# The first unit's gate and up stage in a written order for all engines, with the second unit prepared between its pairs

## The chip, the cores and the metric

The kernel runs on one NeuronCore of a Trainium2 chip. Its time is device microseconds of one execution; before the change it is 2628.86 us, the median of three runs (2623.89 to 2630.57). TensorE (PE in the profile) multiplies, VectorE (DVE), ScalarE (ACT) and GpSimd (POOL) work elementwise, SyncE (SP) issues all of the kernel's data transfers. Each engine takes its instructions in one fixed order and waits on semaphores.

## The reference

```python
mod = (_silu(L0_c) @ L0_wmod).reshape(L0_c.shape[0], 6, 1, -1)
sa, ca, ga, sb, cb, gb = (mod[:, 0], mod[:, 1], mod[:, 2], mod[:, 3], mod[:, 4], mod[:, 5])
...
h = _layernorm(x, axis=-1) * (1 + ca) + sa
x = x + ga * _L0_attn_ref(h)          # softmax over the 2 samples, per feature, then a mix of them
h = _layernorm(x, axis=-1) * (1 + cb) + sb
x = x + gb * _L0_ffn_ref(h, W_gate, W_up, W_down)
# ffn: up = xf W_up^T, gate = silu(xf W_gate^T), y = (gate * up) W_down^T
```

x is 2 samples of 2048 tokens of 1024 features; the hidden width is 2752. All is float32.

## The kernel before

The tokens are worked in 8 units of 256 tokens of both samples (512 columns). A float32 matrix product is made of float16 ones: each operand is scaled by a power of two and split into a high and a low part (`split`, L152: `high` on ScalarE or GpSimd, L148 and L150, then the low part on VectorE, L154), and three products of parts are added (`PARTS`). From the second unit on, gate and up and the down product run in seven half-size products instead of eight (`gu_pair`, L860; `DN_STEPS`), on sums and differences of blocks of the weights that are prepared once and kept in DRAM: `dgu` for gate and up, `dwd` for down. The first unit meets weights that are not prepared yet.

**Unit 0, gate and up.** The hidden rows go in 11 pairs (`Pair`; the last is half a pair), each with four blocks: gate and up, each in two halves of the contraction. `gu_plain` (L804) multiplies pair p in four steps of 24 matmuls of 512 columns (12 in the last pair), and after each step calls `tick`. That tick makes a block some steps ahead: `block` (L468) splits it into one of five weight tiles (`wtile`) and stores it to `dgu`, odd blocks with the high part on GpSimd. A pair's blocks are read from DRAM four at a time (`load`), a pair's scale needs the largest sum of squares of its blocks: `sums` (Square on ScalarE, L133), `scale_start` (a VectorE maximum), then `laid_out` (L102), a short matmul pa that spreads the maximum over the partitions, then `scale_end` on VectorE (L107 to L121). When m = 0 is multiplied, Silu is taken (L824), when m = 1 is, the product goes to H (L827), and then the sum of its squares is taken.

The same tick also prepares the down weights (`prep_wd`, a generator, one piece at each call): four tiles m, each with four blocks of 640 KB read into `rot`, eight sums of squares, a scale, seven operands (three plain blocks and four sums or differences by `combine`, L429 to L434), each split in two halves into `wt` and `hp` and stored to `dwd`. It reads and multiplies the last section of wmod (`mod_section`), the left-over hidden rows (`prep_left_over`) and the last down rows (`prep_wd_last`).

**Unit 0, down** (L1068 on). Seven steps of 120 matmuls (dX, dY, dZ, L1085), each on an operand of H that `right_dn` forms and splits on ScalarE and VectorE; the sums go back with `add_to`; then pB. Between the steps the next unit is prepared (`prep`, side): z from the unit's x and the statistics `bct` (L650, L651), the attention result (L665 to L669), a mean over the partitions (GpSimd), the deviations and their squares, a root, h. In the last steps the operands of h for the next unit are made (`right_gu`).

**Order.** The text runs up to the third tick of unit 0 under `manual_schedule` for TensorE, VectorE, ScalarE and GpSimd (`in_text`) and for SyncE (`in_order`): there each engine issues in the order of the text. From then on a planner orders each engine's instructions by modelled times, and `issue_after` holds some back. So in unit 0 from about 140 us the order before is the planner's.

## Time and profile before

| What | us |
|---|---|
| Three runs | 2628.86, 2623.89, 2630.57 |
| Profiled execution, its own time | 2624.7 |
| Its span, first to last instruction | 2622.9 |
| First matmul of the gate and up stage of unit 0 (L818) | 116.35 |
| First matmul of its down stage (L1085) | 368.71 |
| First pB of unit 0 (L1111) | 472.96 |
| Granted clock over the span | 0.991 |

Busy time over the span: PE 2556.6 (97%), PEld 2087.5 (80%), DVE 1600.4 (61%), ACT 982.1 (37%), POOL 136.0 (5%). A matmul's end is modelled and matmuls overlap, so a busy TensorE need not be at its peak: the distance from start to start is what counts. An instruction of VectorE starts some 0.07 us before the one in front of it is booked as ended.

### The profile page before, as it was taken

To read this page: it belongs to the slowest core of one execution; us is meant where nothing else is said; L and a number is where in the kernel's file an instruction comes from. 1 tells how busy PE (TensorE), PEld (TensorE's weight loads), DVE (VectorE), ACT (ScalarE), POOL (GpSimd) and SP (SyncE) were. 2 spreads that over 40 slices of the span, in tenths; PEclk is the share of its full clock that TensorE was granted. 3 is DMA by queue.
4 is the path that set the end of the run, shared out by engine and by line. 5 is a ranking of instruction groups with operands and counts; after the bars stand their busy time and mean duration, and the time that the engine had idled before them with its cause. 6 is when DMAs were issued, how large, how long until landed. Compare 5 with 4: busy or idle time off the path is not lost.

```text
span 2622.9 us, 50756 instructions
## 1 busy us (share of the span) xinstructions
PE 2556.6 (97%) x21729; PEld 2087.5 (80%) x21729; DVE 1600.4 (61%) x2659; ACT 982.1 (37%) x1496; POOL 136.0 (5%) x70
## 2 busy tenths in 40 slices
PE   7899898999999999999999999999999999999999
PEld 3344357788887888888887888878887888888887
DVE  8767579866766777493376626584284825622263
ACT  7767564433432454152242423233141413311230
POOL 6211101000000000000000000000000000000000
PEclk9999999999999999999999999999999999999999
DMA  9988765755568766576656666576666666656654
GB/s 390 359 307 320 281 225 174 258 190 193 183 203 293 252 227 216 194 234 201 200 202 225 205 201 200 197 237 201 185 219 218 205 202 202 200 192 202 201 199 152
DMA packets 159010, 586.62 MB, mean 224 GB/s; under 512 B 17216, under 2 KB 17280, under 8 KB 158784
## 3 DMA queue, kind: packets, MB, share of 16 engines
q1 hardware_dynamic: 158784, 583.38, 65.6%
q8 instruction: 170, 2.79, 0.4%
q14 instruction: 56, 0.46, 0.1%
HBM read 506.47 MB, written 76.84 MB: 222 GB/s over the span
## 4 chain that ended last, share of the span: by engine, by line
PE 81%; DMA 8%; DVE 4%; issue 2%; ACT 1%; SPq 0%; DVEq 0%; ACTq 0%
PE pY L875 19%; PE pZ L875 12%; PE pX L875 12%; PE dY L1085 12%; PE dX L1085 8%; PE dZ L1085 7%; PE g L818 3%; PE g L843 3%; PE pB L1111 3%; PE pl L913 1%; DMA out_dram<-big 1%; DMA dwd<-wt 1%; DMA rot<-in_wgp_dram 1%; DMA big<-in_xT_dram 1%; DMA wo<-dgu 1%
## 5 line engine op out<-in xcount | busy, mean ns | idle before, releaser
L875 PEld LDWEIGHTS <-w 128*128 128x128 f16 x8820 | 861.4, 98 | 106.7 <-DMA w<-dgu 3.9
L1085 PEld LDWEIGHTS <-wd 128*128 128x128 f16 x6720 | 658.8, 98 | 88.1 <-issue 6.6
L875 PE MATMUL pY<-hbt,w 128*128 128x256 f16 x3780 | 442.4, 273 | 0.0
L1085 PE MATMUL dY<-rot,wd 128*128 128x256 f16 x2880 | 320.6, 274 | 0.0
L875 PE MATMUL pX<-hbt,w 128*128 128x256 f16 x2520 | 300.6, 273 | 0.0
L875 PE MATMUL pZ<-hbt,w 128*128 128x256 f16 x2520 | 294.4, 273 | 2.8 <-DMA w<-dgu 2.8
L875 PEld LDWEIGHTS <-wo 128*128 128x128 f16 x2688 | 263.4, 98 | 38.0 <-DMA wo<-dgu 4.6
L150 ACT ACTIVATE rot<-H,sA 128x1024 f16<-128x1024 f32 (+1 forms) x168 | 162.8, 1001 | 232.3 <-PE dY L1085 119.8
L818 PE MATMUL g<-hbt,wq 128*128 128x512 f16 x1008 | 226.4, 385 | 11.1 <-ACT wq L150 8.2
L154 DVE SCALAR_TENSOR_TENSOR rot<-H,sA,rot 128x1024 f16<-128x1024 f32 (+1 forms) x168 | 183.0, 1106 | 75.7 <-ACT rot L150 75.3
L1085 PE MATMUL dX<-rot,wd 128*128 128x256 f16 x1920 | 213.7, 273 | 9.4 <-DVE rot L154 5.0
L1085 PE MATMUL dZ<-rot,wd 128*128 128x256 f16 x1920 | 213.5, 273 | 0.0
L818 PEld LDWEIGHTS <-wq 128*128 128x128 f16 x1008 | 99.1, 99 | 134.2 <-ACT wq L150 9.9
L892 DVE TENSOR_TENSOR ev<-pY,e 128x512 f32<-128x512 f32 (+1 forms) x72 | 47.7, 663 | 254.1 <-PE pY L875 252.9
L133 ACT ACTIVATE junk<-H 128x1024 bf16<-128x1024 f32 (+1 forms) x100 | 98.7, 987 | 163.7 <-DVE H L902 146.1
L897 ACT ACTIVATE sil<-ev,inv_f 128x512 f32<-128x512 f32 (+1 forms) x72 | 50.5, 701 | 244.6 <-DVE ev L895 244.3
L875 PE MATMUL pY<-hbt,wo 128*128 128x256 f16 x1152 | 134.6, 273 | 1.5 <-DVE ev L892 1.0
L665 ACT ACTIVATE o<-big,beta,alpha 128x256 f32<-128x256 f32 x112 | 59.8, 592 | 202.3 <-DVE big L651 180.3
L883 DVE TENSOR_TENSOR ev<-pY,e 128x512 f32<-128x512 f32 (+1 forms) x72 | 47.6, 661 | 124.4 <-PE pY L875 124.4
L886 ACT COPY e<-pZ 128x512 f32<-128x512 f32 (+1 forms) x72 | 40.4, 561 | 188.5 <-PE pZ L875 188.4
L843 PE MATMUL g<-hbt,wo 128*128 128x256 f16 x960 | 108.6, 275 | 2.2 <-DMA wo<-dgu 2.2
L843 PEld LDWEIGHTS <-wo 128*128 128x128 f16 x960 | 94.2, 99 | 15.4 <-DMA wo<-dgu 2.5
(298 smaller groups left out, 2728.1 us busy)
## 6 DMA issues: line engine op xcount, KB each, us to landing
w<-dgu SPq DMA_DIRECT2D x350, 512.0 KB, 4.3
wd<-dwd SPq DMA_DIRECT2D x224, 640.0 KB, 3.9
wo<-dgu SPq DMA_DIRECT2D x85, 512.0 KB, 5.1
dgu<-wo SPq DMA_DIRECT2D x40, 512.0 KB, 4.4
rot<-in_wgp_dram SPq DMA_DIRECT2D x38, 512.0 KB, 5.7
dgu<-wq SPq DMA_DIRECT2D x35, 512.0 KB, 6.4
big<-in_wgp_dram SPq DMA_DIRECT2D x32, 512.0 KB, 7.9
out_dram<-big SPq DMA_DIRECT2D x30, 512.0 KB, 3.1
```

The costliest lines, as they stand in the source:

```text
L133: S.activation(jv, src, AF.Square, accum_out=col)
L150: mark["hi"] = S.activation(dst_hi, src, AF.Copy, scale=s)
L154: return V.scalar_tensor_tensor(dst_lo, src, s, dst_hi, ALU.mult, ALU.subtract)
L665: S.activation(o[:, n], z[:, q, 0], AF.Identity, scale=alpha[:, n, 0, q:q + 1], bias=beta[:, n, q:q + 1])
L818: T.matmul(pt[m, f].rearrange("p n c -> p (n c)"), w[:, wa, f, k], hb0[:, ha, 4 * kh + k], start=kh == 0 and k == 0 and j == 0, stop=kh == ...
L843: T.matmul(pt[m, f][:, n], w[:, wa, f, k], hb[:, ((1, 0), (2, 3))[kh][n], ha, k], start=kh == 0 and k == 0 and j == 0 and n == 0, stop=kh ...
L875: T.matmul(pt[a][:, f], w[:, wa, f, k], hb[:, i, ha, k], start=a not in seen, stop=k == 3 and j == 2, skip_group_check=True)
L883: V.tensor_tensor(u2, pt["Y"], e1, ALU.add)
L892: V.tensor_tensor(c22, pt["Y"], e1, ALU.add)
L897: S.activation(sr, u2, AF.Silu, scale=inv)
L1085: T.matmul(acc[a, h][:, j], w[:, k // 5, wa, k % 5], rot16[:, si % 2, ha, k], start=(a, h) not in seen, stop=k == KH - 1 and jj == 2, skip ...
L1111: T.matmul(pB, wt[0:n, k, wa, m, :], hp[0:n, k, ha, :], start=i == 0, stop=i == len(LAST) - 1)
```

## The change

The text order now holds to the end of the gate and up stage of unit 0, for all five engines: `in_text` and `in_order` are closed after `gu_left_over`, and both `issue_after` at that place go. The work of a tick is written out for step t = 4p + i in `later_tick`, by tables: which block is read (`LOADS`, one a step, each pair in a place of its own, `PLACE`), when the down tiles are read, squared, scaled and split (`T_WD`), when z, y and the deviations of unit 1 are made (`second.z`, `Y0`, `Y1`, `DEV`, `ADD`). So the preparation of unit 1 moves from the down stage into these steps, all but its last part: `rest` (b1, sb) stays in the down stage and the root is taken beside the left-over rows. The last down rows (`prep_wd_last`) move from the gate and up stage into the first two down steps.

Squares are taken over two blocks in one instruction (`sums_of_two`, `Down.sums`), and a down operand is split in one instruction of 1280 elements instead of two of 640, and stored in one transfer of 640 KB, in three places in the spare half of `hbt`. Silu, H and its sum of squares are put off (`late`): Silu to the end of its step's work, H behind the first block of the next pair. Tiles `wt`, `hp` and the small evacuation tiles of `gu_pair` become parts of one tile `mix`, and pairs 5, 7 and 9 are read into it. The sums for the last wmod section are multiplied at the ends of steps 4 to 7, from two places in turn. Units 1 to 7 issue the same instructions as before.

```diff
...
-    hp = ct([P, 2, 2, 2 * TU], "hp", F16)
-    wt = ct([P, 2, 2, KB, P], "wt", F16)
+    mix = ct([P, 4 * D + 3 * 2 * TU], "mix")
+    wt = mix[:, 0:2 * D].bitcast(F16).rearrange("p (a b c d) -> p a b c d", a=2, b=2, c=KB)
+    hp = mix[:, 2 * D:3 * D].bitcast(F16).rearrange("p (a b c) -> p a b c", a=2, b=2)
+    ets = {"sil": [0, 1], "e1": [2, 3], "e5": [4]}
...
+        def sums_of_two(self, i):
+            sumsq(self.base[:, 2 * i * self.n:2 * (i + 1) * self.n], self.sq[:, i:i + 1])
...
+    Hf = H.rearrange("p a n c -> p (a n c)")
+    HT = 2 * TU
+    PLACE = {2: big[:, 1], 3: big[:, 2], 4: Hf[:, 12 * HT:20 * HT], 5: mix[:, 0:4 * D], 6: Hf[:, 12 * HT:20 * HT],
+             7: mix[:, 0:4 * D], 8: Hf[:, 14 * HT:22 * HT], 9: mix[:, 0:4 * D], 10: Hf[:, 18 * HT:22 * HT]}
...
+    class Down:
+        def __init__(self):
+            n = self.n = KH * P
+            self.q = [rot[:, i * n:(i + 1) * n] for i in range(4)]
+            self.place = [spare[:, i * n:(i + 1) * n].bitcast(F16).rearrange("p (g h c) -> p g h c", g=2, h=2)
+                          for i in range(3)]
+            self.at = 0
+        def load(self, m, blocks):
+            for i in blocks:
+                Q.dma_start(self.q[i], wd[m][:, i])
+        def sums(self, i):
+            if i == 0:
+                self.sq = small.tile([P, 2], F32, tag="sqd", name="sqd")
+            sumsq(rot[:, 2 * i * self.n:2 * (i + 1) * self.n], self.sq[:, i:i + 1])
+        def scale_start(self):
+            c = small.tile([P, 1], F32, tag="sqc", name="sqc")
+            V.tensor_reduce(c, self.sq, AX.X, ALU.max)
+            return bound(c)
+        def scale_end(self, m, pa):
+            pow2_end(pa, s_wd, inv_wd[:, m:m + 1])
+        def operands(self, m, ids):
+            for i in ids:
+                w = self.place[self.at % 3]
+                self.at += 1
+                src = self.q[{3: 1, 5: 0, 6: 3, 7: 2, **PLAIN}[i]]
+                split(w[:, :, 0], w[:, :, 1], src.rearrange("p (g c) -> p g c", g=2), s_wd)
+                Q.dma_start(dwd[m, i], w.rearrange("p g h c -> p (g h c)"))
...
+    class Second:
...
+        def z(self, ks):
+            nb = [bct[:, i].rearrange("p n c -> p (n c)") for i in range(2)]
+            for k in ks:
+                V.tensor_tensor(self.zf[:, k], self.xf[:, k], nb[1], ALU.add)
...
+            if kh and m == 0:
                 for f in range(nf):
+                    pt["s", f] = evp.tile([P, 2, TU], F32, tag="ev", name="silp", bufs=3)
+                late.append(lambda: [S.activation(pt["s", f], pt[0, f], AF.Silu, scale=inv) for f in range(nf)])
+            if kh and m == 1:
+                late.append(lambda: [V.scalar_tensor_tensor(H[:, 2 * p + f], pt[1, f], inv, pt["s", f], ALU.mult, ALU.mult)
+                                     for f in range(nf)])
+                late.append(lambda: sumsq(H[:, 2 * p:2 * p + nf].rearrange("p f n c -> p (f n c)"), asq[:, p:p + 1]))
...
+            gu_left_over(u, left.w, asq, between=beside_left_over)
+            in_text.close()
+            in_order.close()
+            side = second.rest()
...
+            if u == 0 and si < 2:
+                next(wd_last)
+                if si == 0:
+                    V.tensor_scalar(cB, gbt, iv[1], None, ALU.mult)
...
+            late.pop(0)()
+            w5.extend(mod_load(5, kk, slots_x[2:4]) for kk in range(2))
         if i == 3:
             for b in range(2, 4):
                 pairs[1].block(b)
+            pairs[3] = Pair(3, None, PLACE[3])
+            pairs[3].load(range(4))
+            for b in range(2):
+                pairs[2].sums_of_two(b)
...
+    T_WD = {9 * m + 4: m for m in range(4)}
+    LOADS = {(1, 4 * (q - 3) + b + 1): (q, b) for q in (4, 5, 6, 7, 9) for b in range(4)}
+    LOADS.update({(1, 21): (8, 3), (1, 22): (8, 0), (1, 23): (8, 1), (1, 24): (8, 2), (1, 31): (10, 0), (2, 31): (10, 1),
+                  (1, 32): (10, 2), (2, 32): (10, 3)})
+    Y0 = {17: (0,), 18: (1,), 23: (2, 3), 24: (4, 5), 25: (6,), 26: (7,)}
+    Y1 = {18: (0,), 23: (1,), 24: (2, 3), 25: (4, 5), 26: (6,), 27: (7,)}
+    DEV = {32: (0, 1), 33: (2, 3), 34: (4,), 35: (5,), 36: (6, 7)}
+    ADD = {33: (1,), 34: (2, 3), 35: (4,), 36: (5,), 37: (6, 7)}
+    def later_tick(p, i, asq, s_h, inv_h, right):
+        t = 4 * p + i
+        if i == 0:
+            close, sums_of_h = late[:2]
+            del late[:2]
+            asqs.append(sums_of_h)
+        for l in (1, 2):
+            if (l, t) in LOADS:
+                q, b = LOADS[l, t]
+                if q not in pairs:
+                    pairs[q] = Pair(q, None, PLACE[q])
+                pairs[q].load((b,))
+        m = T_WD.get(t)
+        if m is not None:
+            down.load(m, (0,))
+        m = T_WD.get(t - 1)
+        if m is not None:
+            down.load(m, (1, 2, 3))
+        if t in (5, 6):
+            w5.append(mod_load(5, t - 3, slots_x[2:4]))
+        if 8 <= t < 12:
+            if t == 8:
+                second.stat()
+            second.load(2 * (t - 8))
...
+        if i == 3 and p + 2 <= NP:
+            bounds[p + 2] = pairs[p + 2].scale_start()
+        if i == 0 and t > 4 and p + 1 <= NP:
+            pairs[p + 1].scale_end(pas.pop(p + 1))
+            pairs[p + 1].inv()
+        if t == 4:
+            bounds[2] = pairs[2].scale_start()
+        if t == 5:
+            pairs[2].scale_end(pas.pop(2))
+            pairs[2].inv()
+            pairs[2].block(0)
+        if t > 4 and p + 1 <= NP:
+            pairs[p + 1].block(i)
+        if i == 0:
+            close()
+        if asqs and (i == 3 or t == 40):
+            asqs.pop()()
+        for t0, m in T_WD.items():
+            if t - t0 == 3:
+                down.sums(0)
+            if t - t0 == 4:
+                down.sums(1)
+            if t - t0 == 5:
+                bounds["wd"] = down.scale_start()
+            if t - t0 == 6:
+                down.scale_end(m, pas.pop("wd"))
+                down.operands(m, (4, 1))
+            if t - t0 == 7:
+                down.operands(m, (2,))
+                combine(down.q, 6)
+            if t - t0 == 8:
+                combine(down.q, 5)
+                down.operands(m, (6, 5))
+            if t - t0 == 9:
+                combine(down.q, 3)
+                down.operands(m, (7, 3))
+        if p + 2 <= NP and i in (1, 2):
+            pairs[p + 2].sums_of_two(i - 1)
+        if 14 <= t < 18:
+            second.z((2 * t - 28, 2 * t - 27))
+        second.y_end(Y1.get(t, ()))
+        second.y_start(Y0.get(t, ()))
+        if t == 27:
+            second.total("mean")
+        if t == 29:
+            second.mean()
+        second.add(ADD.get(t, ()))
+        second.dev(DEV.get(t, ()))
+        if t == 37:
+            second.total("var")
+        if t == 39:
+            second.mean()
+            second.root()
+            second.r = tmp.tile([P, 2 * TU], F32, tag="r2", name="r2")
+        if t == 38:
+            left.sums()
+        if t == 39:
+            bounds["left"] = left.scale_start()
+        if t == 40:
+            left.operand(pas.pop("left"))
+        if t == 8:
+            row_of(5)
+        if t == 10:
+            mod_put(5, pts[5])
+            gate(mods[5])
+        if t == 41:
+            c = small.tile([P, 1], F32, tag="cm", name="cm")
+            V.tensor_reduce(c, asq[:, 0:NP], AX.X, ALU.max)
+            bounds["h"] = bound(c)
+        if t == 43:
+            pow2_end(pas.pop("h"), s_h, inv_h)
+            right()
+        if i == 1:
+            late.pop(0)()
+        if t == 9:
+            turn_of(5)
+        for q in (2, p + 2, "wd", "left") + (("h",) if t == 42 else ()):
+            if q in bounds:
+                pas[q] = laid_out(bounds.pop(q))
+        if t in (4, 5, 6, 7):
+            steps_of(5, w5, (t - 4,))
...
+    def beside_left_over():
+        for j in range(7):
+            second.rsqrt(j)
+            if j == 3:
+                for f in late:
+                    f()
...
-        unit(u, iter(()) if last else prep(u + 1), None if last else right_gu(V))
+        unit(u, iter(()) if last or u == 0 else prep(u + 1), None if last else right_gu(V))
```

## The prediction

> **What bounds the kernel now.** I read first the page, then the matmuls of TensorE in order of time over the first unit, then what TensorE waited for in two stretches, and last the other engines there.
>
> The page's slices of 65.6 us (busy tenths; the last row is the granted clock):
>
> ```profile
> PE   7899898999999999999999999999999999999999
> DVE  8767579866766777493376626584284825622263
> PEclk9999999999999999999999999999999999999999
> ```
>
> TensorE is the bound almost everywhere; the dents are in the first seven slices. The change touches the gate and up stage of unit 0 (116.35 to 369) and its down stage (369 to 473). Busy time there:
>
> ```profile
> 116.35:369.00 252.65, 238.48 (x1107) 108.23 (x1108) 169.79 (x291) 170.63 (x287) 32.70 (x20) 0.97 0.75 278
> 369.00:473.10 104.10, 95.39 (x842) 83.68 (x842) 98.26 (x164) 47.45 (x71) 7.41 (x2) 0.97 0.61 214
> ```
>
> The columns are length, PE, PEld, DVE, ACT, POOL, clock, DMA share, GB/s. In the first stretch VectorE has a third of its time free; in the second it has none. The waits show as gaps between matmul groups (start, length, what, idle before):
>
> ```profile
> 133.81 13.11 PE L818 MATMUL g<-hbt,wq 128*128 128x512 f16 x60
> ...
> 299.99 3.60 PE L818 MATMUL g<-hbt,wq 128*128 128x512 f16 x8 [8.20 <-ACT wq L150]
> 305.16 5.35 PE L818 MATMUL g<-hbt,wq 128*128 128x512 f16 x24 [1.57 <-DVE wq L154]
> 310.35 0.39 PE L102 MATMUL pa<-ident,p2b 128*128 128x128 f32 x2
> 310.57 25.85 PE L818 MATMUL g<-hbt,wq 128*128 128x512 f16 x119
> 336.26 0.39 PE L102 MATMUL pa<-ident,p2b 128*128 128x128 f32 x2
> ...
> 350.63 0.49 PE L102 MATMUL pa<-ident,p2b 128*128 128x128 f32 x2 [3.53 <-DVE p2b L113]
> 351.29 11.36 PE L818 MATMUL g<-hbt,wq 128*128 128x512 f16 x44 [0.17 <-DVE wq L154]
> ```
>
> ```profile
> 400.44 0.39 PE L1085 MATMUL dX<-rot,wd 128*128 128x256 f16 x1 [3.71 <-DMA wd<-dwd]
> 400.85 3.95 PE L1085 MATMUL dY<-rot,wd 128*128 128x256 f16 x24
> 408.74 3.38 PE L1085 MATMUL dX<-rot,wd 128*128 128x256 f16 x21 [3.95 <-DVE rot L154]
> ```
>
> From 310.57 to 336.26 are 119 matmuls, 0.216 us each; a step (one block, 24 of them) is 5.18 us. After the 8.20 wait 8 matmuls took 3.60 instead of 1.73: a long wait is paid twice, in the clock too (it stood at 0.50 from 300 to 304).
>
> **What is removed.** Gate and up: waits 8.20 + 1.57 + 3.53 = 13.3; slow matmuls after them 1.9, and 1.7 in the group at 351.29 (11.19 to the next group, 44 x 0.216 = 9.50). Together **16.9 us**. Down: 840 matmuls at 0.1092 (120 in 13.10) are 91.7; from 368.71 to the first pB at 472.96 it is 104.25, so 12.5 lost and 0.67 in front: **13.2 us**. Its cause is VectorE: preparing unit 1 there costs it z 10.0, y 17.0, the deviation 9.7 and the root 5.5, 42 of its 98 us. These leave the stage and 56 remain for 92. What stays or comes (two splits of wd20/wd21 at 1.27, their Squares on ScalarE, the 0.75 MB read just as the weight tiles are fetched) lies beside TensorE. Should the next weight tile be late behind that read, it costs at most what the 3.71 row shows; at best nothing. I leave 2.5 us, so the gain is **10.7**.
>
> **What is added: a written order.** Step t = 4p + i is block i of pair p. Now each engine takes the 44 steps in the order of the text, and the short matmul that spreads a maximum over the partitions (pa, L102) stands at a fixed place on TensorE. Behind a late pa the whole next pair waits. On VectorE a step t cannot run before TensorE has ended step t-1 (five weight tiles, the fifth is that step's), so it gathers no lead; by the end of step 4p+3 it must have started that step's work. So I count VectorE step by step. Prices, as start to next start: low part of a block 1.20 (row 1.28, 0.07 overlap), H 2 x 0.67, scale begun 0.34, scale ended with its factor 1.0 (210.22 to 211.19), the ScalarE high part that must follow before the low 1.1, z 0.61 each, subtraction of down blocks 1.40.
>
> Three prices have no row. A split of 1280 elements: 640 takes 0.87, 1024 takes 1.27, so between 1.27 and 1.74; the line through both gives 1.54, I take 1.47 net. A Square of 2048 or 2560 on ScalarE: 640 is 0.74 and 1024 is 1.04, so 2.0 and 2.4 with the read of the sum, against 2.4 and 3.4 for the separate ones it replaces: ScalarE gains 0.4 to 1 each time. A GpSimd block beside VectorE work:
>
> ```profile
> 181.62 3.02 POOL L148 TENSOR_SCALAR wq<-big,s_gu 128x1024 f16<-128x1024 f32 x1 [11.45 <-DMA big<-in_wgp_dram]
> 183.66 1.66 DVE L154 SCALAR_TENSOR_TENSOR hp<-rot,s_wd,hp 128x640 f16<-128x640 f32 x1
> ```
>
> The split took 1.66 rather than 0.87, GpSimd 3.02 rather than the 1.12 it shows with VectorE idle. Bounds 0 and 0.8 for each odd block; I take 0.5, since some fall into VectorE's pauses.
>
> The Trainium skill (GPSIMD Engine Reference, Key points) says GpSimd shares its SBUF interfaces with VectorE and contends with instructions that have two SBUF inputs. The trace agrees at 183.66. As nearly all of VectorE's work here has two inputs, the rule alone would charge every odd block 0.8, some 6 us more than I do, and it speaks against this change.
>
> Steps 10 to 15, from the end of step 9: 10: 1.2, down scale 2.0 with its ScalarE wait, two splits 2.9, gate of mods[5] 0.6 = 6.7. 11: 0.3 + 1.7 + 1.5 + 2.8 = 6.3. 12: scale 1.0, wait 1.1, 1.2, H 1.3, 1.4, 2.9 = 8.9. 13: 1.7 + 1.4 + 2.9 = 6.0. 14: 1.2 + z 2.4 = 3.6. 15: 0.3. That is 31.8. In front stands 1.8, and at 14 some 2.7, because ScalarE does its share in order too: Silu of the pair waits for TensorE and the next high part stands behind it. 36.3 against six steps with a pa, 31.3: **5.0** before the pa of pair 5. The same count from the end of step 18 (7.0, 8.9, 6.0, 5.5, 0.3, waits 3.7 = 31.4 against 26.1) gives **5.3** before pair 7's; from 27 (9.6, 6.0, 5.5, 0.3, wait 2.5 = 23.9 against 21.0) **2.9** before pair 9's; at 36 the down scale **1.6**, and **0.8** at 18 and 27 together; from 36 to 39 (7.9, 5.5, 6.4 against 15.8) 4.0 before the pa of the left-over, of which the wait at 36 has given about 1, so **3.0**; at 42 **0.5**. Sum 19.1.
>
> The clock adds 1.8 after each of the two long waits (rows 8.20 and 3.53). For the two near 3 the bounds are 0 (row 1.57) and 1.7; nearest is 3.53, but they are shorter, so 0.8 each. Sum 5.2. The Trainium skill (TensorE: Matmul & The Clock Gate, What's actually happening) puts half clock behind an idle window of about 3.4 us; the 0.50 row agrees, and by it the two short ones would cost nothing, 1.6 less.
>
> A further wait is a **transfer**. The third megabyte tile of wmod is issued at step 5 behind the loads of that step, and TensorE needs it after step 6. SP's order from the first store of pair 1 (137.2 in the trace): 3 stores of 512 KB, 2 x 1024, 4 x 512, 640, 512, 3 x 640, 1024: 9728 KB, 9.96 MB. At the 417 GB/s that the trace holds from 256 to 262 this is 23.9 us, plus 1.4 to land (a 256 KB store takes 2.0, 0.6 of it transfer): 162.5. TensorE is there at 139.0 + 3 x 5.18 + 0.2 + two groups of 1.0 = 156.8. **5.7**, and 1.8 in the clock: 7.5. Bounds 0 and 8; I take 7.5, as the queue is full without a break. The other moved loads (xT and stat at steps 8 to 11, a pair's blocks one a step) wait at the head of SP for VectorE's step before, as the stores do; the median for a block of weights is 7.8 us to land in this stretch, and a block is used two or three steps (10 to 15 us) after its issue, so I cost them at nothing. With a VectorE late by a step that cover is down to 5 us, and ScalarE's Squares would wait the missing 3.
>
> ACT's two table loads (Sqrt, then Silu, 1.28 each) move from the down stage to steps 39 and 41 and lie beside the pa waits already counted. Units 2 to 7 issue the same work; their TensorE waits after 473 (14 us in all) I leave as they are.
>
> **Sum.** -16.9 + 19.1 + 5.2 + 7.5 = +14.9 in gate and up, -10.7 in down: +4.2. The profiled execution took 2624.7 (span 2622.9, 1.8 around it), so 2628.9; the median of the three runs is 2628.86, 4.2 above it, so **2633**. What can be told from no change is 0.3%, 7.9 us: 2621 to 2636.7.
>
> **Rivals.** *VectorE keeps up* (30%). For: its 183 us of work (170 less 19 of overlaps, 291 x 0.065, and 3 of fused splits, plus 35, the 42 without the root and overlaps) fit into 231 of matmuls; a few tenths saved in each step undo the pa waits, since each is a difference of two sums near 30. At 5% less and no GpSimd contention 19.1 + 5.2 falls to about 6: 2633 - 18 = **2615**; without the wait on wmod too, 2608. Against: the same steps carry ScalarE's order, and none is free.
>
> *GpSimd and ScalarE slow VectorE's steps* (27%), the slower side. Place: the splits of steps 10-13, 19-22, 28-31, 37-40. With 0.8 for each odd block VectorE loses 0.15 us more a step, with 3% on the rest another 0.15; over 35 steps 10.5, all of it before a pa, plus 2 of clock: **2646**. It decides as soon as VectorE's sum in a pair passes the 21 us of its four steps; pairs 3, 5 and 7 pass it already.
>
> *The down stage does not gain* (6%): its wait moves to wd tiles behind the wd20 read. For: the 3.71 row is such a wait; against: dwd is written long before now. +4 to +8, 2637 to 2641.
>
> **Chances.** Forecast 37%, its own range 2624 to 2641: of it 0.31 within 0.3%, 0.06 slower. First rival 0.28 faster, 0.02 within; second 0.26 slower, 0.01 within; third 0.04 slower, 0.02 within. Faster 0.28, same 0.36, slower 0.36. The range runs from the first rival's lower end, 2608, to the second with the down loss on top, 2652.
>
> **What would show it.** Right: TensorE waits "pa <- DVE p2b" several times in 200-380, one "pm <- DMA wmod" near 157; the first dX some 15 us later than 368.7; the down stage near 94 us to pB, with z, o and acc work before it. Wrong: pa waits under 1 us (then the first rival), the wmod wait absent, or new waits in units 1 to 7 from another order there.

## The result, and the profile after

The changed kernel takes 2649.3 us (median of four runs, 2647.67 to 2651.82), the kernel before beside it 2626.58 (four runs): a ratio of 1.0086, 95% interval 1.0068 to 1.0104. It is slower by 0.9%. The forecast was no change (2633, its own range 2624 to 2641); the time lies outside that and inside the whole range, 2608 to 2652. The second rival (GpSimd and ScalarE slow VectorE's steps, 2646) names the side and the place. The profiled execution took 2648.61, its span is 2646.8.

The page's slices (65.6 us before, 66.2 now; the last row is the granted clock):

```profile
PE   7889889999999999999999999999999999999999
PEclk9999899999999999999999999999999999999999
```

The windows of gate and up and of the down stage of unit 0, from the first matmul of gate and up to the first dX and from there to the first pB (columns as in the prediction):

```profile
116.41:399.70 283.29, 246.31 (x1105) 110.32 (x1105) 212.56 (x326) 168.31 (x200) 35.69 (x22) 0.93 0.72 267
399.70:493.51 93.81, 93.81 (x845) 83.48 (x845) 69.70 (x114) 40.41 (x57) 0.00 (x0) 0.98 0.59 199
```

Between the same instructions, gate and up took 252.36 us before (116.35 to 368.71) and takes 283.29 now, at a clock of 0.93 rather than 0.97. The down stage shrank from 104.25 to 93.81, and TensorE no longer pauses in it (it starts at a slow clock, behind the wait of 2.44 us in front of the first dX). VectorE is busy 212.56 us in the first stage, where it was 169.79: the second unit's preparation has moved there. The 71 us that remain to it are not free, as will be seen.

TensorE's matmuls of the stage in order of time (start, length, what, idle before and who ended it):

```profile
164.81 1.94 PE L196 MATMUL pm<-hbt,csT 128*32 128x512 f32 x8 [6.74 <-DMA hbt<-in_wmod_dram]
...
221.97 0.77 PE L112 MATMUL pa<-ident,p2b 128*128 128x128 f32 x2 [5.05 <-DVE p2b L123]
...
271.51 0.79 PE L112 MATMUL pa<-ident,p2b 128*128 128x128 f32 x2 [5.05 <-DVE p2b L123]
272.10 23.58 PE L928 MATMUL g<-hbt,wq 128*128 128x512 f16 x96
...
322.77 0.80 PE L112 MATMUL pa<-ident,p2b 128*128 128x128 f32 x2 [5.14 <-DVE p2b L123]
...
377.26 0.79 PE L112 MATMUL pa<-ident,p2b 128*128 128x128 f32 x2 [9.19 <-DVE p2b L123]
377.84 10.66 PE L928 MATMUL g<-hbt,wq 128*128 128x512 f16 x36
...
399.70 0.49 PE L1155 MATMUL dX<-rot,wd 128*128 128x256 f16 x3 [2.44 <-DVE H L936]
```

Four waits for pa carry the loss, before pairs 5, 7 and 9 and before the left-over. Each is paid again in the clock: the 96 matmuls after 272.10 take 23.58 us, undisturbed ones 20.88; the 36 after 377.84 take 10.66, where the same 36 take 7.93 in the last run below.

VectorE's busy time in three of the stretches that end in such a wait (length, busy, clock, DMA share, GB/s):

```profile
196.00:221.97 25.97, 22.79 (x26) 0.95 0.87 309
245.60:271.50 25.90, 21.78 (x24) 0.98 0.81 293
296.75:322.77 26.02, 21.69 (x31) 0.98 0.52 201
```

TensorE's four steps are 20.9 us long. VectorE is busy for more than that, and it waits besides, 2.9, 3.9 and 4.0 us in these stretches, nearly all of it for the halves of the splits that ScalarE and GpSimd make (the 4.9 in an expectation below counts one more wait, of 1.0 us, that ends just ahead of the second stretch). The two together are nearly the whole 26 us.

In the stretch before the left-over GpSimd is the one to look at. First its own timeline:

```profile
360.71 3.63 POOL L765 PARTITION_ALL_REDUCE var<-acc  x1 [7.28 <-DVE acc L782]
371.29 0.68 POOL L158 TENSOR_SCALAR wq<-H,s_gu 128x512 f16<-128x512 f32 x1 [6.95 <-issue]
```

Then VectorE's:

```profile
361.15 3.53 DVE L164 SCALAR_TENSOR_TENSOR hbt<-rot,s_wd,hbt 128x1280 f16<-128x1280 f32 x1
...
372.01 0.75 DVE L164 SCALAR_TENSOR_TENSOR wq<-H,s_gu,wq 128x512 f16<-128x512 f32 x1 [4.39 <-POOL wq L158]
```

The all-reduce is shown with 3.63 us, but the block behind it on GpSimd starts 10.58 us after it did, and VectorE waits 4.39 for that block. The split beside the all-reduce takes 3.53 us where most of its shape take 1.55. The other all-reduce, for the mean, starts at 298.75, and GpSimd's next block at 308.88.

What stands between the two is in the rows of the block's line, on GpSimd's own sequencer (POOLq), which do not count as busy:

```profile
L158 POOLq MODIFY_POOL_CONFIG  x2: 98/98/98, 301.9 to 302.0; - x2
L158 POOLq MODIFY_POOL_CONFIG  x2: 98/98/98, 364.3 to 364.3; - x2
```

They come right behind the all-reduces, and each time the block starts 7.0 us later. The result of an all-reduce is out long before that. In the kernel before, where no block and no such row follows, ScalarE reads the mean 4.21 us after its all-reduce began, as it does the variance 3.27 us after (453.86 to 457.13):

```profile
434.50 4.17 POOL L657 PARTITION_ALL_REDUCE mean<-acc  x1 [87.44 <-DVE acc L669]
438.71 0.63 ACT L658 ACTIVATE mean<-mean 128x512 f32<-128x512 f32 x1 [3.91 <-POOL mean L657]
```

So by these rows it is GpSimd's change from the all-reduce back to blocks that holds its queue, and not the all-reduce itself. No run here changes that alone. Where an expectation below says that an all-reduce holds GpSimd for some 10 us, this change is the larger part of it.

### The profile page after: what moved, and what is told of

Read it like the earlier page. It is cut to its first block, busy times and chain, and to the rows that moved or that the text cites. A ratio compares the mean times of both kernels' runs of the same rounds, so it can differ in the third digit from the quotient of the medians.

```text
span 2646.8 us, 50538 instructions
## 1 busy us (share of the span) xinstructions
PE 2566.5 (97%) x21729; PEld 2091.1 (79%) x21729; DVE 1601.0 (60%) x2631; ACT 962.4 (36%) x1384; POOL 131.5 (5%) x70
## 4 chain that ended last, share of the span: by engine, by line
PE 79%; DMA 6%; DVE 4%; issue 1%; ACT 1%; SPq 0%; POOL 0%; DVEq 0%; ACTq 0%
PE pY L985 19%; PE pZ L985 12%; PE pX L985 12%; PE dY L1155 12%; PE dZ L1155 8%; PE dX L1155 8%; PE pB L1185 3%; PE g L953 2%; DMA rot<-in_wgp_dram 2%; PE g L928 2%; PE pl L1023 1%; DMA wl<-dgl 1%; DMA out_dram<-big 1%; DMA w<-dgu 1%; DMA wo<-dgu 0%
## 5 line engine op out<-in xcount | busy, mean ns | idle before, releaser
L985 PEld LDWEIGHTS <-wo 128*128 128x128 f16 x2688 | 264.3, 99 | 40.5 <-DMA wo<-dgu 5.9
L160 ACT ACTIVATE rot<-H,sA 128x1024 f16<-128x1024 f32 x168 | 162.6, 1001 | 238.9 <-PE dY L1155 127.9
L164 DVE SCALAR_TENSOR_TENSOR rot<-H,sA,rot 128x1024 f16<-128x1024 f32 x168 | 182.6, 1100 | 83.8 <-ACT rot L160 83.4
L1002 DVE TENSOR_TENSOR ev<-pY,mix 128x512 f32<-128x512 f32 (+1 forms) x72 | 47.7, 662 | 253.4 <-PE pY L985 252.2
L1007 ACT ACTIVATE mix<-ev,inv_f 128x512 f32<-128x512 f32 (+1 forms) x72 | 50.5, 701 | 246.3 <-DVE ev L1005 245.6
L993 DVE TENSOR_TENSOR ev<-pY,mix 128x512 f32<-128x512 f32 (+1 forms) x72 | 47.6, 661 | 124.1 <-PE pY L985 124.1
L691 ACT ACTIVATE o<-big,beta,alpha 128x256 f32<-128x256 f32 x96 | 51.4, 592 | 195.0 <-DVE big L677 181.3
L1136 DVE SCALAR_TENSOR_TENSOR big<-dY,cA,big 128x256 f32<-128x256 f32 x96 | 41.8, 477 | 113.7 <-PE dY L1155 113.7
L996 ACT COPY mix<-pZ 128x512 f32<-128x512 f32 (+1 forms) x72 | 40.4, 561 | 185.9 <-PE pZ L985 185.8
```

What stands on the lines that cost most here:

```text
L160: mark["hi"] = S.activation(dst_hi, src, AF.Copy, scale=s)
L164: return V.scalar_tensor_tensor(dst_lo, src, s, dst_hi, ALU.mult, ALU.subtract)
L691: S.activation(o[:, n], z[:, q, 0], AF.Identity, scale=alpha[:, n, 0, q:q + 1], bias=beta[:, n, q:q + 1])
L985: T.matmul(pt[a][:, f], w[:, wa, f, k], hb[:, i, ha, k], start=a not in seen, stop=k == 3 and j == 2, skip_group_check=True)
L993: V.tensor_tensor(u2, pt["Y"], e1, ALU.add)
L1002: V.tensor_tensor(c22, pt["Y"], e1, ALU.add)
```

## The experiments

Twelve kernels ran. Ratios are to the kernel before on the same chip, with the 95% interval; the changed kernel's is 1.0086, and 0.001 is 2.6 us. "First dX" is the start of the down stage in the run's profile, 399.70 in the changed kernel; the start of gate and up itself differs between the profiles, from 115.25 to 116.76. The sums of waits for pa are those within gate and up, 25.5 us in the changed kernel (25.6 with one of 0.16 just ahead of it). The intervals of most single runs overlap that of the changed kernel, so there the stage in the profile says more than the median.

**The wmod tiles ahead of the pair's loads in SyncE's queue.**

```diff
@@ first_tick
+            w5.extend(mod_load(5, kk, slots_x[2:4]) for kk in range(2))
         if i == 2:
...
@@ later_tick
+        if t in (5, 6):
+            w5.append(mod_load(5, t - 3, slots_x[2:4]))
         for l in (1, 2):
             if (l, t) in LOADS:
```

> The first two megabyte tiles of the last wmod section are issued right after the stores of pair 0, the third and fourth at the head of steps 5 and 6, ahead of the loads of those steps. Everything else as after the change. Theory (the wait on the third tile is a transfer standing behind 9.7 MB in SP's order): the two waits of 2.2 and 6.7 us and the slow clock behind the second go, about -9 to -11, near 2639; the pa waits stay as they are. Rival (VectorE bounds the stage and used those 9 us to catch up): the pa waits of pairs 4 and 5 grow by what is taken away, -0 to -3, near 2648.

2646.56 us, 1.0068 (1.0053 to 1.0083). The waits for wmod fall from 8.9 to 4.4 us (the first tile is in time, the third still 4.39 late), first dX comes 3.8 earlier (395.89), and the median is 2.7 lower. The waits for pa grow from 25.5 to 28.0 and take part of it back, mostly at the pa of down scales and not at pairs 4 and 5, where the rival had them. The time lies between the two expectations: the tile is a term of its own, and a small one.

**The block behind each all-reduce to ScalarE.**

```diff
-            split(w[:, 0:self.n], w[:, self.n:], self.q[i], self.s, on_pool=i % 2 == 1)
+            split(w[:, 0:self.n], w[:, self.n:], self.q[i], self.s, on_pool=i % 2 == 1 and (self.p, i) not in ((8, 1), (10, 3)))
```

> The high parts of the two odd blocks that stand behind a partition all-reduce on GpSimd (block 1 of pair 8, block 3 of pair 10) go to ScalarE. Theory (GpSimd is held some 10 us by each all-reduce, 360.7 to 371.3 for the second, and the block behind it, then VectorE, then the pa of the left-over wait for it): VectorE's wait of 4.4 us goes, the pa wait of 9.2 falls to 4 to 5, that of pair 9 from 5.1 to about 3.5, -5 to -8 with the clock, near 2643. Rival (the 9.2 is VectorE's own sum of steps 36 to 39): the pa wait stays above 8, less than -2.

2645.23 us, 1.0064 (1.0049 to 1.0079), first dX at 394.82. The pa of the left-over:

```profile
372.36 0.80 PE L112 MATMUL pa<-ident,p2b 128*128 128x128 f32 x2 [5.34 <-DVE p2b L123]
```

It waits 5.34 instead of 9.19, that of pair 9 waits 3.59 instead of 5.14. Two blocks moved off GpSimd's queue are worth some 4 us: what stands behind an all-reduce on GpSimd does come late. The 5 us waits before pairs 5 and 7, which have no all-reduce near, stay (5.06 and 4.81), and small waits before other pa give back 1.4 of the 5.4 us.

**The second unit's preparation back in the down stage.**

```diff
-        if 14 <= t < 18:
-            second.z((2 * t - 28, 2 * t - 27))
...
-            side = second.rest()
...
-        unit(u, iter(()) if last or u == 0 else prep(u + 1), None if last else right_gu(V))
+        unit(u, iter(()) if last else prep(u + 1), None if last else right_gu(V))
```

> The preparation of unit 1 (x and stat loads, z, y, mean, deviations, root) goes back to the down stage, as before the change; the written order, loads and places stay. Theory (two things add up, the lumps of the down weights in a fixed order and the moved work): pa waits are left, 1 to 3 us each for pairs 5, 7, 9 and the left-over, the wmod wait stays, the down stage is back at some 104 us; 2635 to 2643. Rival (the moved work alone makes VectorE too slow): all pa waits under 0.6 us, 2625 to 2630. Rival (the order alone, the moved work fits into pauses): pa waits as after the change, 2657 to 2661.

2666.17 us, 1.0139 (1.0123 to 1.0156): slower than any theory had it, and for a reason that none had. The run does not do what it was made for. VectorE's timeline in gate and up:

```profile
182.00 1.87 DVE L692 SCALAR_TENSOR_TENSOR o<-big,alpha,o 128x256 f32<-128x256 f32 x3 [0.18 <-ACT o L691]
...
262.78 2.15 DVE L164 SCALAR_TENSOR_TENSOR wq<-mix,s_gu,wq 128x1024 f16<-128x1024 f32 x1 [13.27 <-POOL wq L158]
```

L692 is the second unit's preparation. Written behind the ordered text, it belongs to the planner, which put it not into the down stage but early into gate and up, in front of operands that are due; its all-reduces came at 224.97 and 251.65, and VectorE waited 13.27 for the block behind the second. TensorE waited 47.1 us for pa. The question was asked again for part of this work, with its order held, in the last runs below.

**The planner's order from step 4 on**, with all else of the change.

```diff
                 pairs[2].sums_of_two(b)
+            in_text.close()
+            in_order.close()
+            ctx.enter_context(tc.issue_after(mark["h2"].ins))
+            ctx.enter_context(tc.issue_after(last_of_text.ins))
```

> The written order ends where it ended before the change, behind the third tick; the steps, loads, places and moved work stay, and the planner orders each engine from there. Theory (the fixed places of pa and of the wmod sums on TensorE cost the time, not the amount of work): pa waits under 5 us in sum, the down stage stays near 94 us, 2612 to 2632. Rival (VectorE has too much work in this stage, or the transfers come too late, in any order): waits of 20 us and more again, 2640 to 2655.

2652.36 us, 1.0086 (1.0071 to 1.0101): the rival. The written order is not worse than the planner's for this arrangement of the work: the waits only stand elsewhere, as TensorE's timeline shows.

```profile
221.69 34.05 PE L928 MATMUL g<-hbt,wq 128*128 128x512 f16 x151 [7.14 <-DVE wq L164]
...
276.37 0.80 PE L112 MATMUL pa<-ident,p2b 128*128 128x128 f32 x2 [10.82 <-DVE p2c L129]
```

**Each pa one step later.**

```diff
-        if i == 0 and t > 4 and p + 1 <= NP:
+        if i == 1 and t > 5 and p + 1 <= NP:
             pairs[p + 1].scale_end(pas.pop(p + 1))
             pairs[p + 1].inv()
+            pairs[p + 1].block(0)
...
-        for q in (2, p + 2, "wd", "left") + (("h",) if t == 42 else ()):
+        for q in (2, p + 1 if i == 0 else None, "wd", "left") + (("h",) if t == 42 else ()):
```

> Each pair's exponent product pa (pairs 6 to 10) is issued one step of gate and up later, and that pair's operands and three of its loads follow it by a step; the work is the same. Theory: the changed kernel loses its time to exponent products put into TensorE's order before VectorE and ScalarE, which take turns within a step, have the maximum ready (5.05 before pair 5, 5.05 before pair 7, 5.14 before pair 9, 0.53 before pair 8). With a step to spare the waits of pairs 7 to 9 go: 9 to 11 us less gate and up, 2638 to 2641 us. Rival: the engines have too little room in a step, so a wait taken away comes back at the next one, in front of the down operands or of the later operand: within 3 us of the changed kernel, 2646 to 2652 us.

2647.66 us, 1.0084 (1.0069 to 1.0099): the rival. TensorE's timeline has the waits again, at the pa of a down scale, fewer and longer:

```profile
241.16 0.80 PE L112 MATMUL pa<-ident,p2b 128*128 128x128 f32 x2 [7.58 <-DVE p2b L123]
...
297.49 0.80 PE L112 MATMUL pa<-ident,p2b 128*128 128x128 f32 x2 [6.94 <-DVE p2b L123]
```

The sum of the waits for pa is 28.2 us against 25.5. VectorE was not a step late at one place, to be forgiven by a step; it had that much more to do, and the next pa collects it.

**All odd blocks on ScalarE.**

```diff
-            split(w[:, 0:self.n], w[:, self.n:], self.q[i], self.s, on_pool=i % 2 == 1)
+            split(w[:, 0:self.n], w[:, self.n:], self.q[i], self.s)
```

> All odd blocks of the first unit's pairs are scaled on ScalarE in place of GpSimd: 16 to 18 more operations of 1.15 us on ScalarE, and GpSimd is left with the two all-reduces. Theory of the prediction's second rival (GpSimd lengthens VectorE's splits, 1.28 to 1.73 us and 1.55 to 3.5 us where they overlap, and its all-reduce holds the next block some 10 us): VectorE's waits for GpSimd (7.8 us in gate and up) and the lengthened splits go, the wait before the left-over block's product falls from 9.2 to about 5: 2640 to 2645 us. Rival: ScalarE, whose squares end just ahead of each maximum, is the one that is late, and 1.15 us more in every second step makes every product's wait longer: 2650 to 2662 us.

2649.89 us, 1.0089 (1.0073 to 1.0106): within the noise of the changed kernel and at the edge of the rival's range. VectorE's busy time from 180 to 400 falls from 180.39 to 173.58 us and its waits for GpSimd's blocks (10.8 in the changed kernel, counted over these 220 us) go, but VectorE now waits for ScalarE:

```profile
DVE wq L164 <- ACT wq L160: 32.3, 20, 4.2
```

In the changed kernel these are 17.1 us. GpSimd does cost VectorE time, 0.4 us a block by an estimate (6.8 us over the 16 blocks of this window), and ScalarE has none to give for it.

**Less VectorE work, twice.** Both leave operations out. The first run takes 11.0 us off VectorE where the tables put z and y, the second 11.9 us off it in the four stretches in which the down operands are made.

```diff
@@ first run
                 V.tensor_tensor(self.zf[:, k], self.xf[:, k], nb[1], ALU.add)
-                V.tensor_tensor(self.zf[:, k], self.zf[:, k], nb[0], ALU.mult)
...
-                V.tensor_tensor(self.x[:, q], self.x[:, q], o, ALU.add)
@@ second run
             if t - t0 == 8:
-                combine(down.q, 5)
                 down.operands(m, (6, 5))
             if t - t0 == 9:
-                combine(down.q, 3)
                 down.operands(m, (7, 3))
```

> The changed kernel with 16 VectorE operations left out in the preparation of the second unit: the product with the reciprocal root in steps 14 to 17 and the sum of the residual in steps 18 to 27 (8 each of 0.69 us, 11.0 us in all). Its output for that unit is therefore not the reference's. Theory as it stands after the products were moved by a step and only came to wait elsewhere: gate and up of the first unit is now bound by VectorE, whose busy time (180 of 220 us) and its waits for ScalarE's and GpSimd's halves (30 us) fill the stage, so work taken off it comes straight off: 2637 to 2643 us, the waits for products down from 25.6 to about 16. Rival: the places of the products in TensorE's order bind, and each waits for the squares on ScalarE: 2646 to 2650 us.

> The changed kernel with two of the four in-place combinations of each part of the down matrix left out, 8 VectorE operations of 1.48 us, 11.9 us in all; two of each part's seven scaled operands are therefore those of plain blocks, and the output is not the reference's. The amount is that of t1_less_vectore (11.0 us, which moved the median by nothing), but all of it stands in the stretches of four steps (20.9 us) at whose end the products of pairs 5, 7, 9 and of the left-over block wait: there VectorE is busy 22.8, 21.8 and 21.7 us and waits 2.9, 4.9 and 3.9 us for ScalarE's and GpSimd's halves, together about the 26 us that the stretch takes. Theory (VectorE with these waits bounds those four stretches and nothing else): each wait falls by 3.0 us, from 5.05, 5.05 and 5.14 to about 2.1, the left-over's from 9.2 to about 6, 12 us in all: 2635 to 2640 us. Rival (the waits for the other halves fill the gap again, as in t1_less_vectore, or the squares on ScalarE end the wait): 2645 to 2650 us.

The first: 2649.11 us, 1.0084 (1.0068 to 1.0099), first dX 2.4 earlier. The theory as it stood, that VectorE bounds the whole stage, falls: the time is the rival's, though its reason, the squares on ScalarE, shows with only 1.5 us in VectorE's waits. Most of the freed time turned into waits for the other halves of the splits (for ScalarE's 24.2 us instead of 17.1). Only the part that lay inside a bad stretch counted: four z operations stand between 218.8 and 221.5 in the changed kernel, right before the pa of pair 5; two of them are gone, 1.4 us, and that pa waits 3.60 instead of 5.05 (a slower clock behind it took 0.7 of this back).

The second: 2642.93 us, 1.0062 (1.0048 to 1.0076), first dX at 390.36, 9.3 earlier. Its interval still touches the changed kernel's, so the stage in the profile weighs more here than the median; TensorE's timeline:

```profile
219.24 0.46 PE L112 MATMUL pa<-ident,p2b 128*128 128x128 f32 x2 [2.44 <-DVE p2b L123]
...
265.79 0.49 PE L112 MATMUL pa<-ident,p2b 128*128 128x128 f32 x2 [2.52 <-DVE p2b L123]
266.11 20.88 PE L928 MATMUL g<-hbt,wq 128*128 128x512 f16 x96
...
367.93 0.80 PE L112 MATMUL pa<-ident,p2b 128*128 128x128 f32 x2 [8.55 <-DVE p2b L123]
```

Where no all-reduce is near, 3.0 us less work shortens the wait by 2.6 and 2.5, and the matmuls behind the second run at full speed (20.88, not 23.58). Before pair 9 the wait is 4.03 (1.1 less) and before the left-over 8.55 (0.6 less): these two stretches also hold the blocks behind the all-reduces, which the run with the two moved blocks showed to come late. Two waits of 1.60 and 1.01 before pair 8 and the pa of a down scale, 0.53 in all before, give some back. So two of four stretches answered as expected, and that is why the run lands between the two expectations. In these two runs work taken off VectorE counted only in those stretches.

**Several edits together.** Two runs join the wmod tiles, the later pa and H of the last pair ahead of the reciprocals with, in the first, the two blocks behind the all-reduces on ScalarE, and in the second all odd blocks on ScalarE.

> As the run with four edits, but only the two blocks that stand behind the all-reduces go to ScalarE, the other odd blocks stay on GpSimd. Theory: 3 for the modulation tiles, 10 for the products, 2.4 for the multiplications, 4 for the all-reduces: 2628 to 2634 us; the difference to the run with all odd blocks on ScalarE is that of GpSimd's remaining 14 blocks. Rival: less than half of the sum: 2637 to 2648 us.

> Four edits together: modulation tiles ahead of the pair loads in the sync queue, products a step later, the last pair's multiplications ahead of the reciprocals, all odd blocks on ScalarE. Theory: what single edits win adds up, 3 for the modulation tiles, 10 for the products, 2.4 for the multiplications, 4 for the all-reduce: 2628 to 2634 us, level with the kernel before. Rival: the freed time is taken up by the next wait, less than half of the sum: 2637 to 2648 us.

2633.2 us, 1.0032 (1.0019 to 1.0045), in the theory's range, and 2641.0, 1.0060 (1.0045 to 1.0075), in the rival's. In the ratio the first wins 0.0054 over the changed kernel; the single runs won 0.0018, 0.0022 and 0.0002, and the wait for H, whose edit did not run alone, is 0.0009 (2.44 us), together 0.0051. The second is some 7 us behind it by the ratios: GpSimd's other blocks are worth that much where they stand, contention and all.

Last, the version that was to beat both kernels: the edits of the first of these, and the deviations, their squares, the all-reduce, the root and its reciprocals of the second unit behind gate and up, held there by `issue_after` on the first down operand; with the later pa and without.

```diff
         def rest(self):
+            for q in range(0, KB, 2):
+                self.dev((q, q + 1))
+                yield
+                self.add((q, q + 1) if q else (1,))
+            self.total("var")
...
+                    with ExitStack() as behind:
+                        if u == 0:
+                            behind.enter_context(tc.issue_after(mark["lo", 0].ins))
+                            behind.enter_context(tc.issue_after(mark["hi", 0].ins))
+                        for _ in range(4):
+                            run_gen(side)
...
-        if t in (4, 5, 6, 7):
-            steps_of(5, w5, (t - 4,))
+        if t in (4, 5, 7):
+            steps_of(5, w5, {4: (0,), 5: (1,), 7: (2, 3)}[t])
```

> The edits of s3_all except the reciprocals' place, and two more: the deviations of the second unit, the sum of their squares, its all-reduce and its root (15.7 us of VectorE, 5 us of ScalarE) go behind gate and up into the first part of the down stage, and the third modulation tile is multiplied a step later. VectorE is idle for some 20 us at the end of that stage in s3_all, while TensorE never waits there. Theory (VectorE bounds gate and up): 9 us less in gate and up than s3_all and 4 less for the tile, nothing given back in the down stage: 2618 to 2624 us, faster than the kernel before. Rival: VectorE's added 15.7 us delay the rotated operands of the down stage, which TensorE then waits for as it did before the change (9.4 us): 2628 to 2636 us.

> As t2_best, but with each pair's product at its place of the changed kernel, not a step later. Theory (VectorE bounds, the place of a product only says where the wait is seen): within 4 us of t2_best. Rival (in the single run the later place won nothing because the all-reduce's hold took it back, and without that it is worth its 10 us): 8 to 12 us over t2_best.

2629.09 us, 1.0008 (0.9998 to 1.0017), and without the later pa 2631.68, 1.0014 (1.0006 to 1.0023). The first is level with the kernel before and beats it not; the forecast of 2618 to 2624 was too good. The down stage gave nothing back. Its window in the run of four edits, and then in this one:

```profile
386.15:478.29 92.14, 92.14 (x845) 82.62 (x844) 72.43 (x118) 39.55 (x56) 0.00 (x0) 1.00 0.62 212
```

```profile
381.24:473.50 92.26, 92.26 (x846) 82.75 (x845) 83.35 (x131) 46.68 (x67) 4.15 (x1) 1.00 0.62 212
```

VectorE's 11 us more lie wholly beside TensorE. But gate and up won only 4.6 us: the wait before the left-over fell from 7.0 to 3.2, the two before (7.58 and 6.31) are in steps from which nothing was taken, and the wmod tile still comes 4.3 late though it is used a step later. Without the later pa the median is 2.6 us higher, with intervals that overlap: within the 4 us of the theory, and not the rival's 8 to 12.

## Why the prediction was wrong in its size and right in its place

The forecast was some 16 us short, though the time lies inside the whole range. Gate and up against the prediction's sum, in us from the profile:

| Term | Predicted | Measured |
|---|---|---|
| Removed waits and slow matmuls | -16.9 | -16.9, and -0.7 before dX |
| pa of pair 5 | 5.0 | 5.05 |
| pa of pair 7 | 5.3 | 5.05 |
| pa of pair 9 | 2.9 | 5.14 |
| pa of the down scales, at 36 | 1.6 | 0 |
| pa of the down scales, at 18 and 27 | 0.8 | 0 and 0.53 |
| pa of the left-over | 3.0 | 9.19 |
| pa of h | 0.5 | 0.50 |
| clock after pa waits | 5.2 | 10.0 |
| wmod with its clock | 7.5 | 10.6 |
| H before dX | 0 | 2.44 |
| Sum | +14.9 | +30.9 |

The clock row is 1.89 + 2.70 + 2.67 + 2.73, each the matmuls after a wait less as many undisturbed (15.70 for 72, 20.88 for 96, 7.93 for 36). The wmod row is 2.15 + 6.74 of waits and 1.66 of slow matmuls. The wait of 0.53, which an expectation above gives to pair 8, stands behind the maximum of a down scale (L575). The down stage gained 10.4 (104.25 to 93.81), or 11.1 with the 0.67 in front of dX, as the prediction counted its 10.7. Of the 2.1 us left above 91.7, 1.67 are the slow clock behind the wait for H (14.93 for the first 120 matmuls, 13.26 for the next): the 2.5 left for the moved work came out near, for another reason. What follows the first pB took 3.4 longer than before (2153.3 against 2149.9). 30.9 - 10.4 + 3.4 = 23.9, which is 2648.6 from the profiled 2624.7.

**Right.** The order of events: the waits named in the prediction are the ones that came, pa for VectorE several times and one for wmod, and the two that it counted from undisturbed stretches came to within 0.25 us. The mechanism under them stands: the run with the later pa and the two runs with less VectorE work show that VectorE with its waits for the other halves bounds the stretches of the down operands, in the last two together with the late GpSimd blocks, as the second rival put it ("as soon as VectorE's sum in a pair passes the 21 us of its four steps"). The down stage's gain holds too. Its cause, the preparation taken off VectorE there, fits the waits that are gone (of 9.4 us before, 5.0 were for VectorE and 3.7 for a weight tile) but was not tested by itself: with 11 us of that work back there, TensorE did not wait.

**Wrong.** The step that failed is the count of VectorE "from 27" and "from 36 to 39". It laid the deviations' additions and the splits end to end and passed over GpSimd's queue: both all-reduces, which the prediction does not name, stand in these stretches, at steps 27 and 37, with a block behind each that VectorE needs and that starts 10.1 and 10.6 us after the all-reduce began. In the kernel before both ran in the down stage (434.50 and 453.86), with no block behind them on GpSimd, so no row of that stage showed it. The two waits are 8.4 us of the miss (5.14 and 9.19 for 2.9 and 3.0), and the run with the two moved blocks took 5.4 us of it away. The other 3.0 us stay open. The same count had a wait of 1.6 at step 36 that did not come; it had taken 1 off the left-over's for it.

The second term mis-sized is the clock. The two waits "near 3" were given 0.8 each as too short; they turned out long, and pair 9's and the left-over's cost 2.7 each. Pair 7's cost 2.7 instead of 1.8. The third is the wmod transfer, 3.1 short: the first tile, for which the prediction has no term, was 2.15 late, and the third 6.74 where 5.7 was predicted. Last, H of pair 10 before dX was not seen: it stands on VectorE behind the four reciprocals that the change put beside the left-over rows.

```profile
395.61 3.38 DVE L791 RECIPROCAL r<-rs 128x128 f32<-128x128 f32 x4
398.90 0.65 DVE L936 SCALAR_TENSOR_TENSOR H<-g,inv_f,silp 128x512 f32<-128x512 f32 x1
```

In both runs that put H ahead of the reciprocals, together with three other edits, that wait is gone.

**The forecast as a whole.** The likeliest case was the one with the middle prices for what no row showed. The rival had the side and, at 2646, nearly the time, by other sums: 0.15 us more in every step for GpSimd's contention and as much for 3% on the rest, with no all-reduce in it. That it came so near is luck: the 0.4 us a block that the run without GpSimd's blocks gives is not the rival's 0.8 but nearer the forecast's 0.5, and ScalarE then took the time. The first rival's 183 us of VectorE work rest on a misreading: the 169.79 of the window counts overlapping time once already, so the 19 us for overlaps come off twice. Without that it is 202; the changed kernel has 212.56.

**Open.** The 3.4 us after the first pB. In the other kernels that part took 2149.5 to 2157.9 us. TensorE's waits there sum to 14.3 us before and 15.4 after, so they hold only 1.1 of the 3.4; these are single profiles, and runs of one kernel lie up to 6.7 us apart. No run took it apart. Whether moving z and y into the down stage as well would beat the kernel before was not tried.

## What to carry to other kernels

When work is moved between stages, add up each engine's busy time and its waits for partners over the few steps to the next fixed point, not over the stage: a third of VectorE's time was free on average, and four stretches of four steps were overfull. A late maximum is not helped by reading it a step later if the engine that makes it is behind by work; take work out of the stretch. And whatever moves onto an engine's queue, look at the next instruction behind it there and at who waits for that one, above all where GpSimd changes from one kind of work to another.

## What the runs showed of the hardware

A block behind an all-reduce over the partitions starts on GpSimd some 10 us after the all-reduce did, though its record shows a third of that: 298.75 to 308.88 and 360.71 to 371.29 in the changed kernel, with 3.25 and 3.63 us shown; the same distance, 10.4 and 10.6, in the run with less work in the stretches. In between the sequencer has MODIFY_POOL_CONFIG rows, and the block starts 7.0 us after them (7.2 and 7.0 in that run). A reader of the result on another engine does not wait for this: 4.2 and 3.3 us in the kernel before. A split of 1280 elements on VectorE beside an all-reduce took 3.53 us rather than 1.55.

A pause of TensorE is paid a second time in the clock, by an amount that its length does not set. After pauses of 3.2 to 11.7 us in gate and up the pa or wmod product and the matmuls behind it lost 1.6 to 3.3 us in the runs that keep the written order: 2.3 and 3.1 after two pauses of 5.05 us in the changed kernel, 2.6 after 11.68. After 2.52 us, or 1.60 and 1.01 close together, they lost nothing, after one of 2.44 us 1.7. Before the first dX a pause of 2.44 us cost 1.7 in the changed kernel and one of 2.45 nothing in the run with the later pa. The Trainium skill (TensorE: Matmul & The Clock Gate, What's actually happening) has a free-running window of about 3.4 us: an idle one halves the clock, a busy one restores it. An estimate from that page is 3.4 to 6.8 us at half speed, 1.7 to 3.4 lost, and no dependence on the length of the pause. The rows agree with that about, the smallest of 1.6 just under it; the pauses of 2.44 us that cost 1.7 are shorter than the page's window.
